# The end of the last group in a four-layer graph network: new order of the last steps, gate before theta, bias by TensorE, flag read before the last store

## The chip, the cores and the metric

The kernel runs on one core of a Trainium2 chip. The core's engines are TensorE (PE in the profile; PEld is its weight load), VectorE (DVE), ScalarE (ACT), GpSimd (POOL) and SyncE (SP, which issues the transfers here). Each engine works off its own queue in order and waits for the others at semaphores. The metric is the time of one execution on the device in microseconds.

## The reference, cut to what matters

There are 128 graphs of 64 nodes with 256 features each. Four blocks follow one another, each with layer norm ahead of it; `nodemask` is all ones.

```python
# block 0 and 1: attention over the graph with 8 heads, 32 wide
scores = q @ k.T / sqrt(32)           # block 0: masked by adj; block 1: + log(adj + 1e-6)
x = x + softmax(scores) @ v @ Wo + bo
# block 2: gated graph network, 5 steps
m = h @ weight[l];  agg = adj.T @ m
r, z = sigmoid(agg @ w_ih + h @ w_hh + biases)
n = tanh(agg_n + b + r * (h_n + b'));  h = (1 - z) * n + z * h
# block 3: gated mix of a filtered and a plain product
norm = (sum(|adj|) + 1e-6) ** -0.5
f_hom = adj @ (x @ theta * norm) * norm
f_het = x @ W_h
gate = sigmoid(x @ W_t + b_t)
out = x + elu(gate * f_hom + (1 - gate) * f_het)
```

The last lines are where most of the change lies: `theta`, `W_t` and `W_h` are three 256 x 256 matrices, and the elu closes the kernel.

## The kernel before, in words

The 128 graphs are paired into blocks of 128 rows, and four blocks make a group, so there are 16 groups, 0 to 15. A group passes through the front (both attention blocks), five steps of the gated network, and the back (block 3). The groups overlap: while one is in its five steps, the next one's front and the last one's back are mixed in. All arithmetic is float32.

The order on each engine is not written by hand. Every step is recorded with an engine, an estimated cost and the values that it reads and writes; a planner (`Plan.run`) then gives out one step at a time. Steps have a key, their due place in the run: it comes from the strand in which they were recorded (a base and a span, in units of groups) and is pulled forward by what depends on them. Of the steps of an engine that could begin within 15 ns of the first one, the planner takes the one with the lowest key. What it gives out is emitted in that order, and the engines keep it.

The names that matter here:

- `last_step` is the fifth step of the gated network, in token order, with banks `gb`, `nb`, `gc`, `nc` (L1195). For group 15 (`halves`) it finishes blocks 0 and 1, then blocks 2 and 3. Sums from the banks are made on VectorE (L1221), the last product of half 0 goes through ScalarE copies (L1230) and two additions of the bias row (L1233). `update` then does tanh of both gates together (L1254), L1255, L1257, tanh (L1259), L1260, L1265 and L1267, which gives `ht`.
- `back_half` is block 3 for two blocks: x gets `ht` (L1458), then statistics (L587, L588, L548), `rstd` as a power on POOL (L549), `xn` (L593), a transposition on TensorE (`lnT`, L563) and `hT` on ScalarE (L568).
- `plain_products` gives, for each block, `f` = x theta (L1396, copied by VectorE at L1403) and `gate`, a bank with both the gate's and the plain product (L1400, copied by ScalarE at L1404).
- Then, for each block: bias `b_t` (L1476 on POOL for group 15, L1479 on VectorE otherwise), tanh (L1481), `hom`, the filtered product (L1483), and the elementwise steps L1486, L1489, L1491, L1497, L1502, L1504, L1506. L1508 stores two blocks, 256 KB. Group 14's half 0 is left for the end too, and is mixed with group 15.

The first program (`lean`) assumes that no row of the input of block 2 has a variance of exactly zero. A flag says whether that held (written at L1575); if not, a general program runs after it. The flag is read by all engines behind the whole first program:

```python
        network(tc, a, out, flag)
        beyond = nc.values_load(flag[0:1, 0:1])
        with tc.If(beyond > 0, preferred_fallthrough_block=False):
            network(tc, a, out, None)
```

In the built program of before, the blocks of code lie in this order: first program, the waits for the outstanding stores (the way out when the flag is 0), general program, end. The functions that the change touches:

Of the kernel before, what the change touches and what calls it, by code (L numbers as in the profile page):

```python
# [23 lines left out]
P = 128  # L24
# [45 lines left out]
LOCK = 0.26  # L70
BACK_END = 0.1
# [62 lines left out]
class Op:  # L134
    __slots__ = ("eng", "cost", "lat", "fn", "key", "left", "users", "ready", "vals", "port", "mode", "leaves")


class Plan:
# [3 lines left out]
    def __init__(self):  # L142
        self.ops, self.at = [], 0.0
# [10 lines left out]
    def add(self, eng, cost, fn, reads=(), writes=(), lat=None, early=0.0, holds=(), port=False, mode=WIDE, leaves=None):  # L154
# [5 lines left out]
        op.key = self.at - early  # L160
# [47 lines left out]
    def run(self):  # L208
# [12 lines left out]
        for _ in range(len(self.ops)):  # L221
# [3 lines left out]
            for eng, ops in ready.items():  # L225
# [16 lines left out]
                if found:  # L242
                    first = min(at for at, _ in found) + 15
                    small = sum(t[1].mode in (T64, T32) and t[0] <= first + 100 for t in found)
                    pick = min((t for t in found if t[0] <= first),
# [33 lines left out]
def gnn_stack_kernel(tc: tile.TileContext, a: dict, out: bass.AP):  # L279
    nc = tc.nc  # L280
    with tc.tile_pool(name="flag", bufs=1) as keep:
        flag = keep.tile([P, 1], mybir.dt.int32, name="flag")
        network(tc, a, out, flag)
        beyond = nc.values_load(flag[0:1, 0:1])
        with tc.If(beyond > 0, preferred_fallthrough_block=False):
            network(tc, a, out, None)
# [3 lines left out]
def network(ctx: ExitStack, tc: tile.TileContext, a: dict, out: bass.AP, flag):  # L290
# [896 lines left out]
    def last_step(nm, h, Th, Ta, agg, gv, banks, operand, by_both, whole, halves):  # L1187
# [37 lines left out]
        def taken(oc, half, which):  # L1225
            ps = slice(oc, PAIRS, 2) if halves else slice(2 * half, 2 * half + 2)
            for t in range(2):
# [16 lines left out]
        def update(j):  # L1244
# [6 lines left out]
            else:  # L1251
                hh = lambda: ht[:, :, j * P : (j + 1) * P]
                before, to = [(ht, j)], (ht, j)
            sca(act(2 * TOK, 0.4), lambda: nc.scalar.activation(sg.tile, sg.tile, AF.Tanh, scale=0.5), parts, [sg])  # L1254
            vec2(dve(TOK), lambda: nc.vector.scalar_tensor_tensor(  # L1255
                a_(), r(), 1.0, a_(), op0=ALU.add, op1=ALU.mult), [sg, sn], [sn])
# [6 lines left out]
            else:  # L1263
                pool(1230, less(nc.gpsimd), [*before, sn], [sn])
            vec2(dve(TOK), lambda: nc.vector.scalar_tensor_tensor(  # L1265
                b_(), z(), 1.0, b_(), op0=ALU.add, op1=ALU.mult), [sg, sn], [sn])
# [4 lines left out]
        if halves:  # L1271
# [4 lines left out]
            both(4, 0)  # L1276
            taken(1, 0, 0)
            update(0)
            both(5, 1, True)
            summed(1, 1, 1, v)  # L1280
            both(3, 1)
            summed(0, 1, 1, u)
            update(1)
            yield
# [81 lines left out]
    def back(g, xt, norm):  # L1366
# [20 lines left out]
        for half in (0, 1) if g + 1 == n_groups else (1, 0):  # L1387
            back_half(g, xt, adjT, norm, half)

    def plain_products(hT, F, name):  # L1390

        for i in range(2):
# [10 lines left out]
            vec(dve(256), lambda i=i, pf=pf: nc.vector.tensor_copy(F[i][:, 0, :], pf[:, :D]), [pf], [(F[i], 0)])  # L1403
# [49 lines left out]

    def back_half(g, xt, adjT, norm, half):
        h_by_token = final[g]
        for p in range(2 * half, 2 * half + 2):
# [5 lines left out]
        hT = normed(xt, half, f"{g}_3_{half}")  # L1462

        F = [new("F" if g + 2 < n_groups or half else "h" if g + 2 == n_groups else ("kexp", "qk")[i], [P, 3, D], 2, f"F_{g}_{2 * half + i}") for i in range(2)]
        if g + 1 == n_groups or g + 2 == n_groups and not half:
# [3 lines left out]
        for p in range(2 * half, 2 * half + 2):  # L1469
# [5 lines left out]
            if g + 1 == n_groups:  # L1475
# [135 lines left out]
```

## Time and profile before

| | before |
|---|---|
| time, median of 3 runs | 2499.57 us (2499.54 to 2500.3) |
| profiled execution, its own time | 2500.02 us |
| its span, first to last instruction | 2498.1 us |
| mean granted TensorE clock | 0.996 |
| busy: PE / DVE / ACT / POOL | 2472.3 / 1911.6 / 1300.1 / 1009.7 us |
| instructions | 58019 |
| last step on VectorE ends | 2491.19 us |

Times inside the run are microseconds from the first instruction. The span is what the instructions cover; the execution's own time is 1.9 us longer. A busy PE in the profile is not PE at its peak, since products are pipelined and their ends are modelled. In the chain of work that ended last, each piece is what released the next one. In lists of groups, `out<-in` names the tiles, and a releaser is what ended an engine's wait.

### The profile page before, as it was taken

How to read it: one execution, taken by the hardware profiler on the slowest of the kernel's cores; microseconds unless marked ns; L12 is line 12 of the kernel's file. 1: busy time of each engine (PE TensorE's matmuls, PEld its weight loads, DVE VectorE, ACT ScalarE, POOL GpSimd, SP SyncE). 2: the span in 40 equal slices, each digit the busy share in tenths (PEclk: the TensorE clock that was granted, in tenths of full speed). 3: DMA queues.
4: the chain of work that ended last, by engine and by line, in shares of the span. 5: the costliest groups of instructions: out<-in, count | busy, mean ns of one | idle time of the engine just before them, and what ended most of it. 6: DMA issues, size and time to landing. Idle time of an engine off the chain costs nothing.

```text
span 2498.1 us, 58019 instructions
## 1 busy us (share of the span) xinstructions
PE 2472.3 (99%) x23481; PEld 2030.7 (81%) x23481; DVE 1911.6 (77%) x4524; ACT 1300.1 (52%) x2634; POOL 1009.7 (40%) x959
## 2 busy tenths in 40 slices
PE   9999999999999999999999999999999999999997
PEld 7788888887878878788888888878788787887874
DVE  5567787878777787877878778787877878867777
ACT  3355555555555555455555555555554555654544
POOL 5633424435243352533535244352433525234342
PEclk9999999999999999999999999999999999999998
DMA  7422212212222121222213132122222212212210
GB/s 219 155 81 86 75 50 95 77 50 87 72 80 70 62 83 63 80 70 84 76 48 104 50 102 74 55 77 72 80 70 69 73 62 80 74 49 70 72 50 19
DMA packets 88603, 191.45 MB, mean 77 GB/s; under 512 B 23603, under 2 KB 77189, under 8 KB 77445
## 3 DMA queue, kind: packets, MB, share of 16 engines
q1 hardware_dynamic: 88208, 187.59, 22.5%
q8 instruction: 188, 3.08, 0.5%
q14 instruction: 91, 0.74, 0.1%
q10 hardware_dynamic: 116, 0.04, 0.0%
HBM read 169.58 MB, written 18.02 MB: 75 GB/s over the span
## 4 chain that ended last, share of the span: by engine, by line
PE 97%; DVE 2%; ACT 1%; POOL 0%; issue 0%; DMA 0%; DVEq 0%; ACTq 0%
PE gb L1013 18%; PE gc L1013 13%; PE nb L1013 9%; PE nc L1013 7%; PE qkvb L727 6%; PE qkvc L727 5%; PE y L895 4%; PE nb L1195 3%; PE agg L1058 3%; PE gb L1195 3%; PE l3b L1425 3%; PE s L791 3%; PE gc L1195 3%; PE nc L1195 2%; PE l3c L1425 2%; PE hT L563 2%
## 5 line engine op out<-in xcount | busy, mean ns | idle before, releaser
L1127 POOL TENSOR_TENSOR sn<-h,sn 128x512 f32<-128x512 f32 x128 | 164.4, 1284 | 542.2 <-ACT sn L1125 542.2
L815 POOL TENSOR_TENSOR e<-e,mask 128x512 f32<-128x512 f32 x128 | 170.2, 1342 | 237.9 <-ACT e L813 237.9
L982 POOL TENSOR_TENSOR Th<-h 128x256 f32<-128x256 f32 x160 | 125.5, 803 | 272.4 <-PE nb L1013 133.1
L1013 PE MATMUL gb<-Ta,gv 128*128 128x256 f32 x768 | 199.0, 381 | 0.3 <-DVE Ta L1071 0.3
L1013 PE MATMUL gb<-Th,w_hh 128*128 128x256 f32 x768 | 197.4, 380 | 0.7 <-DVE sg L1090 0.7
L549 POOL TENSOR_TENSOR rstd<-pw,few 128x2 f32<-128x2 f32 x128 | 114.2, 892 | 206.3 <-DVE pw L548 202.9
L1013 PEld LDWEIGHTS gb<-Ta,gv 128*128 128x128 f32 x768 | 141.5, 190 | 21.9 <-DVE Ta L1071 0.7
L1125 ACT ACTIVATE sn<-sn,b_n 128x512 f32<-128x512 f32 x128 | 92.1, 720 | 129.1 <-DVE sn L1123 127.6
L1013 PEld LDWEIGHTS gb<-Th,w_hh 128*128 128x128 f32 x768 | 140.3, 190 | 20.1 <-issue 1.2
L1071 DVE TENSOR_TENSOR Ta<-agg 128x256 f32<-128x256 f32 x160 | 93.9, 589 | 79.5 <-ACT sg L1117 37.0
L1129 DVE SCALAR_TENSOR_TENSOR sn<-sg,sn 128x512 f32<-128x512 f32 x128 | 115.8, 905 | 45.9 <-POOL sn L1127 45.1
L982 POOL TENSOR_TENSOR Th<-h,Th 128x256 f32<-128x256 f32 x160 | 134.9, 843 | 8.9 <-DVE h L1131 5.9
L895 PE MATMUL y<-w_L_gnn_Wo,oT 128*128 128x256 f32 x512 | 133.3, 380 | 0.1
L1013 PE MATMUL gc<-h,w_hh 128*128 128x256 f32 x512 | 131.9, 380 | 0.1
L1013 PE MATMUL gc<-agg,gv 128*128 128x256 f32 x512 | 131.4, 379 | 0.0
L804 POOL TENSOR_TENSOR x<-x,r_L_gnn_bo 128x512 f32<-128x512 f32 x64 | 89.4, 1397 | 77.9 <-DVE xn L593 52.5
L568 ACT ACTIVATE hT<-lnT 128x512 f32<-128x512 f32 x96 | 57.2, 596 | 116.9 <-PE lnT L563 116.9
L1064 ACT ACTIVATE agg<-agg 128x512 f32<-128x512 f32 x160 | 86.6, 593 | 58.9 <-PE agg L1058 58.8
L1013 PE MATMUL nb<-Th,w_hh 128*128 128x256 f32 x384 | 116.1, 384 | 0.0
L1013 PE MATMUL nb<-Ta,gv 128*128 128x256 f32 x384 | 114.5, 380 | 0.0
L727 PEld LDWEIGHTS qkvb<-hTQ,qw 128*128 128x128 f32 x696 | 100.0, 191 | 16.6 <-DVE v L748 0.8
L1090 DVE TENSOR_TENSOR sg<-gc,ug 128x512 f32<-128x512 f32 x64 | 43.8, 685 | 89.4 <-PE gc L1013 88.2
(286 smaller groups left out, 7122.9 us busy)
## 6 DMA issues: line engine op xcount, KB each, us to landing
gv<-gates SPq DMA_DIRECT2D x80, 1344.0 KB, 5.8
qw<-kept SPq DMA_DIRECT2D x203, 192.0 KB, 2.4
x<-in_x_dram SPq DMA_DIRECT2D x32, 256.0 KB, 3.6
out_dram<-x SPq DMA_DIRECT2D x32, 256.0 KB, 2.2
gates<-gv SPq DMA_DIRECT2D x5, 1344.0 KB, 5.1
adjq<-in_adj_dram SPq DMA_DIRECT2D x8, 256.0 KB, 3.5
adjblk<-in_adj_dram SPq DMA_DIRECT2D x32, 64.0 KB, 2.3
gw<-in_L_gnn_weight_dram SPq DMA_DIRECT2D x5, 256.0 KB, 6.8
```

Source lines behind the costliest of these rows:

```text
L549: pool(660 if n == 2 else 970, lambda: nc.gpsimd.tensor_tensor(dst.tile, s.tile, few[:, 1 : 1 + n], op=ALU.pow), [s, (few, 1)], [dst], port=2)
L727: nc.tensor.matmul(bk[:, j * P : (j + 1) * P], lhs, rhs, start=first and j == 0, stop=True, skip_group_check=True)
L815: pool(1225, lambda e=e: nc.gpsimd.tensor_tensor(e.tile, e.tile, bias_at(pp)[:, None, :].to_broadcast([P, 4, 2 * NODES]), op=ALU.mult), [e ...
L895: pe(mm(256), lambda i=i, c=c: nc.tensor.matmul(py[:, i * D : (i + 1) * D], oT[:, i, c, :], w_o[:, c, :], start=c == 0, stop=c == 1), [(oT ...
L982: pool(690, lambda: nc.gpsimd.tensor_tensor(T[:, i, :], x(), y(), op=ALU.subtract), reads, [(T, i)])
L1013: nc.tensor.matmul(bank_[:, col * HALF : (col + 1) * HALF], at(g, n), rhs(), start=first and j == 0, stop=True, skip_group_check=True)
L1071: vec2(dve(256), lambda: nc.vector.tensor_tensor(Ta[:, i, :], x(), y(), op=ALU.subtract), reads, [(Ta, i)])
L1125: sca(act(TOK, 1.5), lambda: nc.scalar.activation(a_(), a_(), AF.Tanh, bias=b_n[:, oc : oc + 1]), [n_v, b_n], [n_v])
L1127: pool(1230, lambda: nc.gpsimd.tensor_tensor(b_(), hh(), a_(), op=ALU.subtract), [*hp, n_v], [n_v])
L1129: vec2(dve(TOK), lambda: nc.vector.scalar_tensor_tensor(b_(), z(), 1.0, b_(), op0=ALU.add, op1=ALU.mult), [*ts[1], n_v], [n_v])
L1195: pe(mm(384), lambda t=t, bk=bk: nc.tensor.matmul(bk[:, P:] if of_h else bk[:, : 3 * P], b()[:, t * P : (t + 1) * P], w[:, :, n, :], start ...
L1425: pe(mm(384), lambda: nc.tensor.matmul(bk[:, : 3 * P], b(), w3[:, :, n, :], start=first, stop=True, skip_group_check=True), [w3, *reads], ...
```

## The change

The change concerns group 15, the part of group 14 that is left for the end, and the way out of the program.

- The two halves of group 15's back are recorded in strands of their own (`END`, `END_SPAN`), and steps recorded with `plan.wait = 200` let the planner take a step with a lower key even where it can begin only up to 200 ns after the first possible one. This is set for `taken`, `update` and the norm of group 15's back.
- The last product of half 0 in `last_step` is added to its bias row directly from the bank by VectorE, and tanh of r and of z are two instructions.
- `last_half` takes the place of the products and elementwise steps for group 15: the bias goes into the gate's bank by a product with a column of the identity; both blocks' gate products come ahead of both blocks' theta products; tanh and the plain product are read from the bank; `part` = (1 - gate) * plain and (1 + tanh) * norm are made apart, so that after `hom` there are one product, one addition, exp, and two steps onto x, from which 1 has been taken before. Half 0's `f` is copied by ScalarE, half 1's by VectorE.
- Group 14's half 0 uses the same formula with the bias still on POOL, its `f` copied by ScalarE.
- The last store is split: block 2, then block 3. The flag is read ahead of the last store, and the general program's code lies ahead of the waits for the stores (`preferred_fallthrough_block=True`). The built order of code is: first program, general program, waits for the stores, end.

```diff
+END = 1.85, 1.9
+END_SPAN = 0.5, 0.5
+ENDS = 1
+WAIT = 200
...
-                    first = min(at for at, _ in found) + 15
-                    small = sum(t[1].mode in (T64, T32) and t[0] <= first + 100 for t in found)
-                    pick = min((t for t in found if t[0] <= first),
+                    first = min(at for at, _ in found)
+                    small = sum(t[1].mode in (T64, T32) and t[0] <= first + 115 for t in found)
+                    pick = min((t for t in found if t[0] <= first + t[1].wait),
                                key=lambda t: t[1].key + self.shift(mode, t[1].mode, small))
...
-        network(tc, a, out, flag)
-        beyond = nc.values_load(flag[0:1, 0:1])
-        with tc.If(beyond > 0, preferred_fallthrough_block=False):
+        beyond = network(tc, a, out, flag)
+        with tc.If(beyond > 0, preferred_fallthrough_block=True):
             network(tc, a, out, None)
...
+            for t in range(2) if halves else ():
+                bk, p = banks[which][t], 2 * t + oc
+                for dst, part in zip(s[half], (slice(1, 3), slice(0, 4, 3))):
+                    vec(dve(256), lambda dst=dst, part=part, bk=bk, p=p: nc.vector.tensor_tensor(
+                        dst[:, p], bk.tile.rearrange("p (g f) -> p g f", g=4)[:, part, :], b_row[:, oc, part, :], op=ALU.add),
+                        [bk, b_row], [(dst, p)])
+            if halves:
+                return
...
+            rz = [(sg, k) for k in "rz"] if halves else [sg, sg]
+            if halves:
+                for k in range(2):
+                    sca(act(TOK, 0.4), lambda k=k: nc.scalar.activation(
+                        sg[:, :, k, :], sg[:, :, k, :], AF.Tanh, scale=0.5), parts, [rz[k]])
+            else:
+                sca(act(2 * TOK, 0.4), lambda: nc.scalar.activation(sg.tile, sg.tile, AF.Tanh, scale=0.5), parts, [sg])
...
+            plan.wait = WAIT
             taken(1, 0, 0)
             update(0)
+            plan.wait = 15
...
-        for half in (0, 1) if g + 1 == n_groups else (1, 0):
+        if g + 1 == n_groups:
+            return adjT
+        for half in 1, 0:
...
-            vec(dve(256), lambda i=i, pf=pf: nc.vector.tensor_copy(F[i][:, 0, :], pf[:, :D]), [pf], [(F[i], 0)])
+            sca(act(256), lambda i=i, pf=pf: nc.scalar.activation(F[i][:, 0, :], pf[:, :D], AF.Copy), [pf], [(F[i], 0)])
...
+    def last_half(g, xt, hT, F, adjT, norm, half):
+        blocks = range(2 * half, 2 * half + 2)
+        pg, pf = ([new_(f"{n}_{g}_{p}") for p in blocks] for n, new_ in (("gate", gate), ("f", bank)))
+        for p in blocks:
+            sca(act(256, 0.4), lambda p=p: nc.scalar.activation(
+                xt[:, p, :], xt[:, p, :], AF.Copy, bias=-1.0), [(xt, p)], [(xt, p)])
+        for i in range(2):
+            pe(mm(256), lambda i=i: nc.tensor.matmul(
+                pg[i][:, :D], ident[:, 0:1].to_broadcast([P, P]), b_t.tile, start=True, stop=True,
+                skip_group_check=True), [ident, b_t], [pg[i]], holds=[F[i]])
+        for i in range(2):
+            for kc in range(2):
+                pe(mm(512), lambda kc=kc, i=i: nc.tensor.matmul(
+                    pg[i].tile, hT[:, kc, i * P : (i + 1) * P], w3[:, 1:, 2 * kc : 2 * kc + 2, :], start=False, stop=True,
+                    skip_group_check=True), [hT, w3], [pg[i]])
+        for i in range(2):
+            for kc in range(2):
+                pe(mm(256), lambda kc=kc, i=i: nc.tensor.matmul(
+                    pf[i][:, :D], hT[:, kc, i * P : (i + 1) * P], w3[:, 0, 2 * kc : 2 * kc + 2, :],
+                    start=kc == 0, stop=kc == 1), [hT, w3], [pf[i]])
+        for i, p in enumerate(blocks):
+            f, gt = (lambda i=i, k=k: F[i][:, k, :] for k in range(2))
+            sca(act(256, 0.4), lambda i=i, gt=gt: nc.scalar.activation(gt(), pg[i][:, :D], AF.Tanh, scale=0.5),
+                [pg[i]], [(F[i], 1)])
+            if half:
+                vec(dve(256), lambda i=i, f=f: nc.vector.tensor_copy(f(), pf[i][:, :D]), [pf[i]], [(F[i], 0)])
+            else:
+                sca(act(256), lambda i=i, f=f: nc.scalar.activation(f(), pf[i][:, :D], AF.Copy), [pf[i]], [(F[i], 0)])
+            pe(mm(256), lambda i=i, p=p, f=f: nc.tensor.matmul(
+                pf[i][:, D:], adjT[:, p, :], f(), start=True, stop=True), [adjT, (F[i], 0)], [pf[i]])
+            part = new("cp", [P, D], 5, f"part_{g}_{p}")
+            sca(act(256, 0.4), lambda gt=gt, part=part: nc.scalar.activation(
+                part.tile, gt(), AF.Copy, scale=-0.5, bias=0.5), [(F[i], 1)], [part])
+            vec(dve(256), lambda i=i, part=part: nc.vector.tensor_tensor(
+                part.tile, pg[i][:, D:], part.tile, op=ALU.mult), [pg[i], part], [part])
+            sca(act(256, 2), lambda p=p, gt=gt: nc.scalar.activation(
+                gt(), gt(), AF.Identity, scale=norm[:, p : p + 1], bias=norm[:, p : p + 1]),
+                [(F[i], 1), norm], [(F[i], 1)])
+            o = new("o", [P, D], 2, f"o3_{g}_{p}")
+            vec(dve(256), lambda i=i, o=o, gt=gt: nc.vector.scalar_tensor_tensor(
+                o.tile, pf[i][:, D:], 0.5, gt(), op0=ALU.mult, op1=ALU.mult), [pf[i], (F[i], 1)], [o])
+            vec2(dve(256), lambda o=o, part=part: nc.vector.tensor_tensor(
+                o.tile, o.tile, part.tile, op=ALU.add), [o, part], [o])
+            sca(act(256, 0.4), lambda o=o, gt=gt: nc.scalar.activation(gt(), o.tile, AF.Exp), [o], [(F[i], 1)])
+            vec2(dve(256), lambda p=p, o=o: nc.vector.scalar_tensor_tensor(
+                xt[:, p, :], o.tile, 0.0, xt[:, p, :], op0=ALU.max, op1=ALU.add), [o, (xt, p)], [(xt, p)])
+            vec2(dve(256), lambda p=p, gt=gt: nc.vector.scalar_tensor_tensor(
+                xt[:, p, :], gt(), 1.0, xt[:, p, :], op0=ALU.min, op1=ALU.add), [(F[i], 1), (xt, p)], [(xt, p)])
+        if not half:
+            dma(256, lambda: nc.sync.dma_start(
+                out_t[:, g * PAIRS : g * PAIRS + 2, :], xt[:, :2, :]), [(xt, 0), (xt, 1)], [])
+            return
+        dma(128, lambda: nc.sync.dma_start(out_t[:, g * PAIRS + 2, :], xt[:, 2, :]), [(xt, 2)], [])
+        ends.append((xt, 3))
+        if not lean:
+            last_store()
...
-        if g + 1 == n_groups or g + 2 == n_groups and not half:
+        if g + 1 == n_groups:
+            last_half(g, xt, hT, F, adjT, norm, half)
+            return
+        if g + 2 == n_groups and not half:
             plain_products(hT, F, f"{g}_{half}")
...
+            if ENDS and g + 2 == n_groups and half == 0:
                 pool(650, lambda gt=gt: nc.gpsimd.tensor_tensor(gt(), gt(), b_t.tile, op=ALU.add),
                      [(v, 0), (v, 1), b_t], [(v, "gt")])
...
+                part = new("cp", [P, D], 5, f"part_{nm}")
+                sca(act(256, 0.4), lambda gt=gt, part=part: nc.scalar.activation(
+                    part.tile, gt(), AF.Copy, scale=-0.5, bias=0.5), [(v, "gt")], [part])
+                pool(690, lambda het=het, part=part: nc.gpsimd.tensor_tensor(
+                    part.tile, het(), part.tile, op=ALU.mult), [part, (v, 0), (v, 1)], [part])
+                sca(act(256, 2), lambda p=p, gt=gt: nc.scalar.activation(
+                    gt(), gt(), AF.Identity, scale=norm[:, p : p + 1], bias=norm[:, p : p + 1]),
+                    [(v, "gt"), norm], [(v, "gt")])
+                vec(dve(256), lambda o=o, ph=ph, gt=gt: nc.vector.scalar_tensor_tensor(
+                    o.tile, ph[:, :D], 0.5, gt(), op0=ALU.mult, op1=ALU.mult), [ph, (v, "gt")], [o])
+                vec2(dve(256), lambda o=o, part=part: nc.vector.tensor_tensor(
+                    o.tile, o.tile, part.tile, op=ALU.add), [o, part], [o])
+                sca(act(256, 0.4), lambda o=o, gt=gt: nc.scalar.activation(gt(), o.tile, AF.Exp), [o], [(v, "gt")])
+                vec2(dve(256), lambda p=p, o=o: nc.vector.scalar_tensor_tensor(
+                    xt[:, p, :], o.tile, 0.0, xt[:, p, :], op0=ALU.max, op1=ALU.add), [o, (xt, p)], [(xt, p)])
+                vec2(dve(256), lambda p=p, gt=gt: nc.vector.scalar_tensor_tensor(
+                    xt[:, p, :], gt(), 1.0, xt[:, p, :], op0=ALU.min, op1=ALU.add), [(v, "gt"), (xt, p)], [(xt, p)])
+                continue
...
+    read = []
+
+    def last_store(known=None):
+        xt, p = ends.pop()
+
+        def go():
+            if lean:
+                read.append(nc.values_load(flag[0:1, 0:1]))
+            nc.sync.dma_start(out_t[:, n_pairs - PAIRS + p, :], xt[:, p, :])
+
+        dma(128, go, [(xt, p)] + ([known] if lean else []), [])
+
+    ends = []
...
-                back(g, *held.pop(g))
+                xt, norm = held.pop(g)
+                adjT = back(g, xt, norm)
+            for half in range(2) if last else ():
+                with plan.strand(begin[g] + END[half], END_SPAN[half]):
+                    back_half(g, xt, adjT, norm, half)
...
+        with plan.strand(n_groups + 2.0, 0.1):
+            last_store(known)
     plan.run()
+    return read[0] if lean else None
```

## Prediction

> **What bounds the kernel now.** First the page's chain of work that ended last, by engine:
>
> ```profile
> PE 97%; DVE 2%; ACT 1%; POOL 0%; issue 0%; DMA 0%; DVEq 0%; ACTq 0%
> ```
>
> TensorE carries it, and the listed orders of instructions of the two kernels are the same on every engine until the last 60 us, two ScalarE steps near 2435 apart. So only the end can change. A table of that end by windows (window, its length, then busy us of PE, PEld, DVE, ACT, POOL; granted clock; DMA share and GB/s):
>
> ```profile
> 2430.00:2460.00 30.00, 29.89 (x164) 18.36 (x163) 24.91 (x50) 16.07 (x32) 15.66 (x13) 1.00 0.03 10
> 2460.00:2470.00 10.00, 4.23 (x14) 2.20 (x12) 9.40 (x25) 3.53 (x6) 1.75 (x1) 0.94 0.00 0
> 2470.00:2480.00 10.00, 9.28 (x27) 5.80 (x28) 6.51 (x21) 3.46 (x7) 1.55 (x3) 0.72 0.08 29
> ```
>
> Until 2460 PE is full; from 2460 to 2470 it idles, VectorE is full (9.40 of 10), and the clock pays afterwards (0.72). What fills those 10 us, from the chain in order of time (start, us, what):
>
> ```profile
> 2462.83 0.06 DVE x L1458
> ...
> 2467.69 1.76 POOL rstd L549
> ...
> 2471.20 0.61 ACT hT L568
> ...
> 2471.85 2.07 PE f L1396 x4
> 2473.92 2.65 PE gate L1400 x4
> 2476.58 0.86 PE f L1396 x4
> 2477.44 1.72 PE gate L1400 x4
> ...
> 2480.71 1.13 PE f L1396 x4
> ...
> 2486.14 0.45 PE hom L1483 x2
> ...
> 2490.77 0.42 DVE x L1506
> ```
>
> The same f and gate groups take 4.72 us after the idle stretch and 2.58 later. After the last hom (2486.59) 4.6 us of elementwise work remain, until 2491.19. Then the exit (engine and operation of a line: durations in ns, first to last start):
>
> ```profile
> L1508 SPq DMA_DIRECT2D out_dram<-x x32: 372/389/394, 370.7 to 2491.2; - x32
> ...
> L284 SPq TENSOR_LOAD <-flag x1: 479/479/479, 2491.6 to 2491.6; - x1
> ...
> L285 SPq COMPARE_BRANCH  x2: 43/46/49, 2492.2 to 2494.2; - x2
> ...
> L1607 SPq EVENT_SEMAPHORE  x10: 17/28/28, 2496.8 to 2498.1; - x10
> ```
>
> Last store, flag, a branch that falls through, the waits for the stores (2.9 us to landing in the DMA view of 2490 to 2500), then at 2494.2 a branch over the fallback network: SP's next instruction is at 2496.8, 2.5 us later. From the last DVE end (T = 2491.2) to the span's end: 6.9 us.
>
> **The change part by part.** I walk the listed order of each engine with durations of before. Units: PE 0.43 us for a 256-column product, 0.65 for 384, 0.86 for 512; DVE 0.42 for 256 elements (next start after 0.34), 0.68 for 512 (after 0.60, a dependent one after 0.78); ACT 0.42, 0.63 (512, tanh); POOL pow 0.71; PE's result reaches DVE or ACT 0.2 after its slot, other hand-overs 0.04 to 0.1.
>
> *GRU, half 0.* The pairs L1195 are permuted, not changed: they end at 2455.63 as before, the last gb and nb 0.65 earlier, at 2453.05 and 2453.69. Removed: four ACT copies (L1230) and two DVE additions of 512. Added: four DVE additions from the bank, 2453.3 to 2454.7. Tanh of r alone ends at 2455.0 (before: 1.06 us for both, to 2456.74). Then L1255 2455.06, L1257 2455.84, tanh 2456.56 to 2457.19, L1260 2457.45 behind three sums of half 1, L1265 2458.23, L1267 2459.01: ht at 2459.7 against 2462.5. The x, statistics and pow's input of half 0 now stand directly behind: x 2459.95 and 2460.35, statistics from 2460.76, pow's input done 2461.9 (before 2467.6, because update and products of half 1 were mixed in), rstd 2462.7.
>
> *What is passed over.* The four sums of half 1 (L1221, from u) stand after that; nc ends 1.7 us later than before (2462.1 against 2460.4), since two bias products (0.86) and theta's (0.86) are ahead of it, and the sums end at 2463.4. xn at 2463.3 and 2463.65, lnT at 2464.7 to 2465.1. The other two bias products reuse gc's and nc's banks, so they wait for those sums, and lnT is queued behind them; the sums end before xn, so this costs nothing; were the sums later, lnT would move with them one for one. All four bias products (1.7 us) lie before PE's wait for half 0; without that cover they cost 1.7. Group 14's POOL addition stands ahead of rstd: it ends at 2461.5, 0.4 before rstd is wanted.
>
> *hT of half 0* stands on ACT behind two subtractions on x15 (which wait for xn) and a copy of group 14: 2465.45 to 2466.05. PE idles 0.6, then gates 3.44, theta 1.72, hom of group 14 0.43, two hom 0.86, with 0.1 to restart: 2472.6. The f group starts at 2471.85 before, this gate group at 2466.1: 5.7 us earlier, and with no idle stretch near the 3.4 us that led to the 0.72 clock.
>
> *Half 1.* r's tanh 2463.5, L1255 2464.05, L1257 to 2465.53, but its tanh stands on ACT behind hT of half 0 and runs 2466.05 to 2466.68; L1260 2466.72, L1265 2467.5, L1267 to 2469.0, x and statistics to 2470.95, rstd 2471.8, xn to 2472.8 (one addition and one product of other blocks before it, in rstd's shadow), lnT to 2473.4, two subtractions on ACT, then hT to 2474.05. PE is done with half 0 at 2472.6, so both engines arrive about together, and an error of half a microsecond on either shows. Gates of blocks 2 and 3 to 2477.6, theta to 2479.4, the last copy 2480.0, the last hom 2480.55. Before, each of these blocks went gate copy 0.60, POOL bias 0.72, tanh 0.42, and after hom L1486, L1489, L1491, L1497, L1502, L1504, L1506, seven steps. Now tanh reads the bank, and part and the factor with norm are done under theta; the gate's second half is multiplied straight from the bank. After the last hom: product 2480.96, addition 2481.69 (between steps of the block before), exp 2482.2 to 2482.6, last step 2482.7: T = 2483.1. Two terms I raise: pow at its mean 0.89 instead of the median 0.71 (+0.18, for half 1 alone: half 0's has 0.6 to spare), a restart after a gap by 0.27 as in the 1.13 against 0.86 (+0.17). T = 2483.5, 7.7 earlier.
>
> *ACT's added work* (two subtractions, a copy, part, per block) lies in gaps of an engine with 3.5 busy us in 10; group 14's two, placed near 2435 ahead of an l5 copy, cost 0 to 0.8, where DVE's user of that copy comes much later: 0. The copies of theta moved from DVE to ACT: 0 net.
>
> *Exit.* The flag was written at 2332.5, so SP's load of it ahead of the last store waits for nothing and vanishes behind the wait for x; the other engines load it after their last step, as before. The second store of group 14 and the two earlier ones of group 15 stand ahead on SP, and their data are done by 2480.5. The last store carries 128 KB instead of 256. The blocks are swapped: fallback first, the waits for stores behind it. The branch at T + 0.5 now jumps, 2.5 us, while the store lands (2.2 to 2.9 from T): T + 3.0; eight semaphores at 0.073, T + 3.6; the end block follows in line, 1.3 as before: T + 5.0, 1.9 less. DVE's jump takes longer (2491.6 to 2495.0, 3.4) and ends at T + 3.6, within that. No row shows this order: bounds are a second jump (+2.5, so 0.6 worse than before) and a store and jump in full overlap with the semaphores (2.5 better); I take 1.9, by the rows of both pieces. [...] The row has 0.05 where it falls through and 2.5 where it jumps. [...] Before has such a jump too, after the landing, so the count stays one.
>
> *Sum.* Span 2483.5 + 5.0 = 2488.5. The profiled run is 2500.02 for a span of 2498.1 (1.9 outside): 2490.4, and it lies 0.45 over the median of the three runs, 2499.57: 2490.0.
>
> **Rivals.** *Early start lost* (chance 0.12). POOL or ACT in front of rstd or hT of half 0 is late, and PE begins near 2471.85 with the cold 2.1 us. Then 2471.85 + 2.1 + 12.0 of both halves' products + 0.9 (hom of group 14, lnT) + 0.3 waiting for the last copy gives the last hom at 2487.1, and the 2.55 behind it T = 2489.7: 2496.1, of the gain only tail and exit. For it: DVE steps beside POOL's two-input ones stretch (L1491 955 ns mean instead of 420). Against: POOL has only 4 x 0.72 and two pow there, so at most 4.3 us.
>
> *Exit gains nothing or jumps twice* (0.10): 0 to 0.6 over before's exit, 2491.9 to 2492.5. For it: no run shows the layout. Against: one branch of before falls through at 0.05.
>
> *Slow clock* (0.03), the other side: PE has several short waits from 2463 on, and the clock stays at about half for the whole last stage, as in the f group's 2.07 against 0.86. The stage holds some 13 us of products; at half rate T = 2496, 2502.5. It decides once the slow work passes 10 of those 13 us. Against: the gap of 2.4 us at 2463.5 cost the next hom nothing, and mine are below 1 us.
>
> That the change does not do what it says is out: the listed order shows every move.
>
> **How the numbers follow.** Forecast 0.75 (2488 to 2493), the rivals 0.12, 0.10, 0.03. Measurement tells 0.2%, 5.0 us, from no change: 2494.6. Forecast and exit rival lie below it; of the lost start three quarters lie above: same 0.09. Slower needs over 2504.6: the slow clock's upper part and what I do not see, 0.02. Range 2487.5 to 2494.5: lower end if every raised term and the full exit overlap go my way, upper end towards the lost start.
>
> **What would show it.** Right: lnT of group 15's half 0 near 2465, gate of its block 0 near 2466, granted clock near 1 from 2465 to 2480, the last DVE step near 2483.5 with SP's end block 3.7 later. Wrong: PE waiting over 3 us for hT, rstd behind a late POOL step, two jumps on SP, or an end of the L1195 pairs after 2456.

## The result, and the profile after

| | before | after |
|---|---|---|
| time, median of 5 runs each | 2499.57 us | 2488.49 us (2488.33 to 2489.63) |
| ratio | | 0.9957, 95% interval 0.9942 to 0.9971 |
| profiled execution, its own time / span | 2500.02 / 2498.1 us | 2488.33 / 2486.5 us |
| last step on VectorE ends (T) | 2491.19 us | 2481.34 us |
| T to the end of the span | 6.9 us | 5.15 us |
| write of the flag to the end of the span | 165.6 us | 155.7 us |

The changed kernel is 11.1 us faster; 2490.0 was forecast. The last row is the better measure of the change. The after trace runs 1.67 us ahead of the before trace from about 11 us on, long before anything that the change touches, and keeps that lead as far as the flag (written at 2332.5 and 2330.8). So of the 11.6 us between the two spans 1.67 belong to the start, told at the end, and about 10 to the change. Put on the scale of before, T is 2483.0.

The stretches of the end again, in the table by windows (busy us of PE, PEld, DVE, ACT, POOL; granted clock; DMA share, GB/s):

```profile
2460.00:2470.00 10.00, 9.75 (x35) 5.83 (x34) 9.25 (x24) 9.22 (x21) 3.88 (x5) 1.00 0.09 29
2470.00:2480.00 10.00, 8.16 (x29) 4.64 (x27) 9.15 (x26) 6.01 (x15) 0.23 (x1) 1.00 0.16 55
2480.00:2492.00 12.00, 0.00 (x0) 0.00 (x0) 1.23 (x4) 0.42 (x1) 0.00 (x0) 0.80 0.09 29
```

TensorE's hole is gone (9.75 busy of 10 instead of 4.23), the clock stays at 1.00 (0.72 before), and TensorE is done before 2480. The chain in order of time (start, us, what):

```profile
2462.30 0.86 PE gate L1484 x4
2463.16 0.45 PE lnT L566 x4
...
2463.64 0.61 ACT hT L571
...
2464.29 3.70 PE gate L1489 x8
2467.99 1.73 PE f L1494 x8
...
2471.64 0.61 ACT hT L571
...
2472.29 3.70 PE gate L1489 x8
2475.99 1.74 PE f L1494 x8
...
2477.76 0.42 DVE F L1502
...
2480.91 0.43 DVE x L1523
```

Each half takes 5.4 us of products at full clock, one `hT` of 0.6 us ahead of each, and 3.2 us of VectorE steps follow the last copy of theta (L1502). The exit (engine and operation of a line: durations in ns, first to last start):

```profile
L1630 SPq TENSOR_LOAD <-flag x1: 512/512/512, 2480.9 to 2480.9; - x1
...
L1631 SPq DMA_DIRECT2D out_dram<-x x1: 348/348/348, 2481.5 to 2481.5; - x1
...
L288 SPq EVENT_SEMAPHORE  x8: 17/17/17, 2484.6 to 2485.1; - x8
...
L288 PEldq COMPARE_BRANCH  x1: 3585/3585/3585, 2478.8 to 2478.8; - x1
...
L288 SPq COMPARE_BRANCH  x1: 45/45/45, 2481.9 to 2481.9; - x1
```

There is one branch per engine instead of two. SP's jumps at 2481.9, while the last 128 KB are under way, and SP goes on at 2484.6; the eight waits for stores behind it, 17 ns each, find everything landed. The load of the flag did not vanish wholly: it stands behind block 2's store, which waits for block 2's last step, so the last store leaves 0.2 after T.

### The profile page after: what moved, and what is told of

Same layout as the page of the kernel before. It is cut to its first block, busy times and chain, and to the rows that moved or that the text cites. A ratio compares the mean times of both kernels' runs of the same rounds, so it can differ in the third digit from the quotient of the medians.

```text
span 2486.5 us, 58043 instructions
## 1 busy us (share of the span) xinstructions
PE 2470.6 (99%) x23489; PEld 2030.3 (82%) x23489; DVE 1906.9 (77%) x4518; ACT 1302.6 (52%) x2644; POOL 1006.8 (40%) x959
## 4 chain that ended last, share of the span: by engine, by line
PE 97%; DVE 1%; ACT 1%; issue 0%; POOL 0%; DMA 0%; DVEq 0%; ACTq 0%
PE gb L1016 18%; PE gc L1016 13%; PE nb L1016 9%; PE nc L1016 7%; PE qkvb L730 6%; PE qkvc L730 5%; PE y L898 4%; PE nb L1198 3%; PE agg L1061 3%; PE gb L1198 3%; PE l3b L1448 3%; PE s L794 3%; PE gc L1198 3%; PE nc L1198 3%; PE l3c L1448 2%; PE hT L566 2%
```

## The experiments

The first four kernels are the kernel before with one part of the change, the others the changed kernel with one part undone or moved. The kernel before ran beside each batch, on three chips: medians 2499.07 (49 runs, beside e1 to e4), 2499.07 (21, beside e5 to e8) and 2498.64 (9, beside e9 to e12). The changed kernel ran in none of these batches, and the intervals of e6 to e12 overlap its own (0.9942 to 0.9971). So a difference of about 1 us between two of these kernels is read from the traces; the medians only hint at it.

The span of every run is known, and its median leaves out the time around the span (1.8 to 2.4 us). The last two columns are read from the one trace of each kernel, count from the write of the flag, and so leave the start out; T is again the end of the last VectorE step. "Flag to end" also contains SP's last jump, which took between 2.6 us (before) and 3.5 us (e7) from trace to trace, so for the work ahead of the exit "flag to T" is the better measure.

| kernel | median us (runs) | median span | ratio, 95% interval | flag to T | flag to end |
|---|---|---|---|---|---|
| before | 2499.07 (49) | 2497.2 | | 158.7 | 165.6 |
| changed | 2488.49 (5) | 2486.6 | 0.9957, 0.9942 to 0.9971 | 150.5 | 155.7 |
| e1_exit | 2497.13 (13) | 2495.3 | 0.9994, 0.9986 to 1.0002 | 158.6 | 164.2 |
| e2_layout | 2497.49 (13) | 2495.7 | 0.9995, 0.9987 to 1.0003 | 158.4 | 164.2 |
| e3_urgent | 2498.76 (13) | 2497.0 | 1.0000, 0.9991 to 1.0008 | 160.4 | 167.7 |
| e4_form | 2495.49 (21) | 2493.6 | 0.9986, 0.9979 to 0.9993 | 155.0 | 161.3 |
| e5_no_urgent | 2493.72 (15) | 2491.9 | 0.9979, 0.9971 to 0.9987 | 154.7 | 160.4 |
| e6_theta_first | 2489.16 (5) | 2487.1 | 0.9960, 0.9946 to 0.9974 | 151.2 | 156.4 |
| e7_no_sums | 2489.46 (5) | 2487.7 | 0.9961, 0.9948 to 0.9975 | 151.4 | 157.5 |
| e8_warm | 2491.25 (7) | 2489.4 | 0.9969, 0.9958 to 0.9981 | 153.3 | 158.7 |
| e9_bias_dve | 2489.46 (5) | 2487.4 | 0.9965, 0.9952 to 0.9979 | 150.5 | 156.2 |
| e10_old_exit | 2490.01 (5) | 2487.7 | 0.9964, 0.9951 to 0.9978 | 150.5 | 157.0 |
| e11_bias_later | 2488.78 (5) | 2486.7 | 0.9961, 0.9947 to 0.9974 | 150.3 | 155.7 |
| e12_start | 2489.48 (5) | 2487.1 | 0.9962, 0.9949 to 0.9976 | 150.5 | 155.7 |

### The exit alone, and its layout alone

The kernel before, with the changed layout and, in e1_exit only, the flag loaded in `network` ahead of the last store (of 256 KB here). e1_exit:

```diff
-        network(tc, a, out, flag)
-        beyond = nc.values_load(flag[0:1, 0:1])
-        with tc.If(beyond > 0, preferred_fallthrough_block=False):
+        beyond = network(tc, a, out, flag)
+        with tc.If(beyond > 0, preferred_fallthrough_block=True):
```

In e2_layout the last line alone is changed.

> The kernel before with the way out of the change alone: flag read ahead of the last store (still 256 KB), general program's code ahead of the waits for stores. Counted from the flag's write on VectorE to the end of the span, before has 165.6 us (2332.5 to 2498.1) and the changed kernel 155.7. Theory (the 2.5 us jump now runs beside the store's landing): from the last DVE end to the end of the span 5.1 us in place of 6.9, so 163.8 from the flag's write, 1.8 us of time. [...] Rival 2 (a second jump is needed behind the waits): 166.2.

> The kernel before with the general program's code ahead of the waits for stores, and the flag read behind the last store as before. Theory: SP issues the store until T + 0.4, loads the flag until T + 0.9, jumps until T + 3.6, waits through eight semaphores until T + 4.2, end block 1.3: T + 5.5 in place of 6.9, so 164.2 us from the flag's write, and 0.4 of the exit's 1.8 us are the flag's place. Rival (the gain is the flag's place, the code's order gives nothing): 165.6, no change.

Both end 1.4 us sooner from the flag (1.9 and 1.6 by the medians, each of whose intervals reaches 1, no change). From T to the end e1 takes 5.7 and e2 5.8, where before takes 6.9, so most of the gain is the layout. What the flag's place adds is open: reading it ahead moved SP's branch from 1.0 to 0.5 after T, but in these two traces the jump then took 3.3 us instead of 2.9, and both spans end at 2495.1. By the medians e1 is 0.4 ahead, the size that was expected, with runs of each spread over 2 us.

### The order alone

The kernel before, with `plan.wait` at 200 around `update`, x and `normed` of group 15, and the halves' own strands:

```diff
+            plan.wait = WAIT
...
+                with plan.strand(begin[g] + END[half], END_SPAN[half]):
+                    back_half(g, xt, adjT, norm, half)
```

> The kernel before with the order by urgency alone: strands of their own for the last group's two halves and the planner's wait of 200 ns; formulas, bias on POOL, gate after theta and exit as before. Theory (the 10 us of idle PE were an order of VectorE's queue that mixes half 1's update into half 0's norm): lnT of half 0 some 4 us earlier than 2470.0, granted clock near 1 after it, last DVE step 4 to 5 us earlier: 160.6 to 161.6 us from the flag's write. Rival (TensorE's products of the last stage are what fills the end, and the formulas shorten it): 164.6 to 165.6.

Missed by both theories: nothing gained in the median, and 2.1 us lost in the profiled execution, which was the slowest of its 13 (2500.53; the range begins at 2497.01). The order does what it says: `lnT` of half 0 starts at 2462.8, as in the changed kernel. But the gain is given back at the end, as a timeline of the last stretch shows:

```profile
2481.85 1.89 PE L1603 MATMUL hom<-F,adjT 128*128 128x256 f32 x8
...
2482.48 0.92 DVE L1606 SCALAR_TENSOR_TENSOR o<-hom,norm,F 128x256 f32<-128x256 f32 x2 [1.73 <-PE hom L1603]
...
2486.97 0.87 DVE L1606 SCALAR_TENSOR_TENSOR o<-hom,norm,F 128x256 f32<-128x256 f32 x2
...
2490.64 0.76 DVE L1626 SCALAR_TENSOR_TENSOR x<-o,x 128x256 f32<-128x256 f32 x2
```

With the old formulas the planner puts the four `hom` products of group 15 (two records each) behind all products of half 1. So the closing steps of all four blocks stand in one row on VectorE, 8.9 us from 2482.5 to 2491.4, where before only two blocks were left behind the last `hom` (4.5 us). And TensorE, though early, runs slow twice:

```profile
2460.00:2470.00 10.00, 8.08 (x22) 4.32 (x21) 9.59 (x28) 3.79 (x6) 0.95 (x2) 0.83 0.00 0
2470.00:2480.00 10.00, 8.15 (x24) 4.78 (x23) 5.78 (x16) 3.98 (x10) 1.87 (x3) 0.83 0.05 16
```

Each half begins with eight products in 4.3 us that take 2.6 at full clock, 1.7 lost each time. The thirteen runs lie in three groups: one at 2497.01 (mean clock 0.998), nine from 2498.59 to 2499.0 (0.997) and three from 2500.35 to 2500.53 (0.996 or 0.997). They lie about 1.7 us apart, the loss of one slow stretch, which fits no such stretch, one and two; only the slowest run has a trace, so that is an estimate.

### The formulas alone, and everything but the order

e4_form is the kernel before with `last_half`, the shortened steps of group 14's half 0 and the sums straight from the banks; order and exit stay. e5_no_urgent is the changed kernel with the planner's 15 and the old strand for both halves:

```diff
-WAIT = 200
+WAIT = 15
...
-        if g + 1 == n_groups:
-            return adjT
-        for half in 1, 0:
+        for half in (0, 1) if g + 1 == n_groups else (1, 0):
```

> The kernel before with the formulas of the change alone: last_half, group 14's half 0, sums straight from the bank, tanh of r and z apart; planner's wait, strands and exit as before. Theory: the tail behind the last hom 2.0 us shorter, the update up to 1 us shorter, the start of half 0 otherwise where it was: 162.6 to 163.6 us from the flag's write. Rival (the formulas carry the change, because they take VectorE and POOL steps out of the 10 us of idle PE): 158 to 159.

> The changed kernel with its order undone: the steps of the last group's update, normalisation and halves take their places as in the kernel before, the new formulas and the new exit stay. Measure: from the write of the flag on DVE to the span's end, 155.7 us in the changed kernel, 165.6 before. Theory A, order and formulas need each other: as in the run of the formulas alone, the gates of half 0 start about 4 us later, TensorE idles 3 us ahead of them and the clock then takes 5.2 us for 3.5 us of products. 161.3 of that run less 1.4 for the exit: 159.9, and a time near 2493.5. Rival B, each part is worth what it gave alone (order 0.3): 156.0, time near 2488.9.

e4 came out between its theory and the rival, 4.4 us better than before from the flag. Its theory gave half 0 at most 1 us of an earlier start; in the trace half 0's products start 1.7 us sooner, counted from the flag. The trace also flatters it: this execution (2494.06) was one of the fastest of 21 (median 2495.49, highest 2497.49), and its clock is at half for 3.4 us where that of before is for 6.8.

e5 is near its theory A in both numbers. So the order, worth 0.3 us by the medians in the kernel before, is worth 5.2 in the changed one (2493.72 less 2488.49), or 4.2 from the flag to T: the parts do not add. The chain of e5 (L1496 gate):

```profile
2468.84 5.12 PE gate L1496 x8
...
2477.08 3.49 PE gate L1496 x8
```

Counted from the flag, half 0 starts 4.2 us later than in the changed kernel (2468.84 less 2331.2, against 2464.29 less 2330.8), and its gate products take 5.12 us where half 1's take 3.49.

### The idle stretch filled

e5_no_urgent, plus turns in the transposition that gives `lnT`:

```diff
         def turn():
+            for _ in range(26 if name == "lnT_15_3_0" else 0):
+                nc.tensor.transpose(ps[:, :P], ident.tile, ident.tile)
```

> The kernel of the undone order (e5) plus 26 turns of the unit matrix on TensorE (2.8 us at full clock, 0.107 each) into the bank of half 0's lnT, right ahead of that lnT and overwritten by it. It adds only work in the idle stretch. Theory A, the slow gate products behind the stretch come from the idle TensorE: with it filled, the gate products of half 0 run at 0.43 each and the end comes 1.6 to 1.8 us sooner than in e5: 158.2 from flag to end, time near 2491.8. Rival B, the slow products come from what VectorE or the banks do there: as e5, or later by what the turns push lnT.

The chain of this kernel (its L1498 is the gate line):

```profile
2464.22 2.84 PE lnT L567 x26
...
2468.65 3.70 PE gate L1498 x8
```

Theory A holds in kind. Turns that compute nothing new stand in the hole, the gate products behind them start at the same time as in e5 and take 3.70 instead of 5.12. What slowed them was TensorE's own idle time. The mean clock is 0.999 in six of the seven runs, and 0.998 or less in all fifteen of e5. T comes 1.4 us sooner than in e5, which is what the gate products gained; the end comes 1.7 sooner, 0.3 of it from a shorter jump of SP (by the medians 2.5). So of the 4.2 us to T that the order is worth, 1.4 are the clock and 2.8 the earlier start itself.

### Theta first; the sums by copies; the bias on VectorE

In e6_theta_first the two loops of `last_half` change places:

```diff
-        for i in range(2):
-            for kc in range(2):
-                pe(mm(512), lambda kc=kc, i=i: nc.tensor.matmul(
-                    pg[i].tile, hT[:, kc, i * P : (i + 1) * P], w3[:, 1:, 2 * kc : 2 * kc + 2, :], start=False, stop=True,
-                    skip_group_check=True), [hT, w3], [pg[i]])
         for i in range(2):
             for kc in range(2):
                 pe(mm(256), lambda kc=kc, i=i: nc.tensor.matmul(
                     pf[i][:, :D], hT[:, kc, i * P : (i + 1) * P], w3[:, 0, 2 * kc : 2 * kc + 2, :],
                     start=kc == 0, stop=kc == 1), [hT, w3], [pf[i]])
+        for i in range(2):
+            for kc in range(2):
+                pe(mm(512), lambda kc=kc, i=i: nc.tensor.matmul(
...
```

In e7_no_sums `taken` and `update` keep their old way for `halves` (the copies on ScalarE, two additions of 512, one tanh):

```diff
-            if halves:
-                return
...
-            if halves:
-                for k in range(2):
-                    sca(act(TOK, 0.4), lambda k=k: nc.scalar.activation(
-                        sg[:, :, k, :], sg[:, :, k, :], AF.Tanh, scale=0.5), parts, [rz[k]])
```

In e9_bias_dve the bias products go, the gate products start their banks themselves, and VectorE adds:

```diff
-                pg[i][:, :D], ident[:, 0:1].to_broadcast([P, P]), b_t.tile, start=True, stop=True,
...
-            sca(act(256, 0.4), lambda i=i, gt=gt: nc.scalar.activation(gt(), pg[i][:, :D], AF.Tanh, scale=0.5),
-                [pg[i]], [(F[i], 1)])
+            vec(dve(256), lambda i=i, gt=gt: nc.vector.tensor_tensor(gt(), pg[i][:, :D], b_t.tile, op=ALU.add),
+                [pg[i], b_t], [(F[i], 1)])
+            sca(act(256, 0.4), lambda gt=gt: nc.scalar.activation(gt(), gt(), AF.Tanh, scale=0.5),
+                [(F[i], 1)], [(F[i], 1)])
```

> The changed kernel with theta's four products ahead of the four gate products in both halves of the last group, all else as changed. Theory A: in half 1 the gates' banks are full 1.7 us later, tanh, part and the factor with norm then stand behind the last product instead of beside theta, and the last VectorE step moves by 0.8 to 1.5: from flag to end 156.7, time near 2489.5. Rival B: the end is bound by VectorE's own steps (9.15 us busy of the 10 from 2470), which stay as many: 155.7, no change.

> The changed kernel with the sums of the update's half 0 as before: ScalarE copies the banks, VectorE adds, one tanh for r and z together. Theory A: ht of half 0 comes 2 to 2.8 us later, TensorE idles so long ahead of the gates of half 0, and the clock may fall behind it: from flag to end 157.7 without a fall of the clock, 159.5 with it; time 2490.5 to 2492.3, I take 2491.5. Rival B: the chain through ht has that much slack against pow and the earlier groups' steps: 156.2 at most.

> The changed kernel with the bias of the last group's gates added by VectorE from the bank into SBUF (four steps of 256 elements), tanh reading that, and no bias products on TensorE. Theory A: the four products of TensorE lie beside other work and cost nearly nothing, while VectorE (9.2 busy us of 10 in both stretches from 2460 to 2480) has no room: four steps of 0.34, one of them between the last gate bank and its tanh, and the end comes 0.3 to 1.0 later: time near 2489.1 against 2488.5. Rival B: the two products right ahead of half 0's lnT hold it for 0.6 (xn is ready at 2462.4, lnT starts at 2463.0), and without them the end comes 0.4 sooner: near 2488.1.

**e6** is 0.7 slower by the medians, at T and at the end: theory A, a little under its lower bound of 0.8.

**e7** is 1.0 slower by the medians and 0.9 later at T. The 1.8 from flag to end have another 0.9 in them from SP's jump, which took 3.5 us in this one execution where it took 2.6 in the changed kernel. Theory A had 2 to 4, B 0.5. `ht` of half 0 came only 1.3 later, and `xn` only 0.5: in the changed kernel `rstd` is ready at 2460.9, but `xn` stands on VectorE behind sums of half 1 until 2461.6, while in e7 it follows `rstd` directly (2462.0 and 2462.1). `lnT` comes 0.4 later, and the clock did not fall (1.00).

**e9** is 1.0 slower in the median. Two of its five runs are 1.4 us or more above the others at a mean clock of 0.998, which is also that of e11's profiled execution with its slow start, so the median says little. In the trace half 0's gates start 1.0 sooner than in the changed kernel, as rival B said, but 0.8 of that is lost again before half 1's, and T is the same. The end is 0.5 later: the last step of block 2 is now late, SP's load of the flag stands behind block 2's store, and so the last store leaves 0.7 after T instead of 0.2. Theory A has the sign, but the loss that the trace shows lies in the exit and not on VectorE; B's 0.6 is there without reaching the end.

### The old exit in the changed kernel

```diff
-        with tc.If(beyond > 0, preferred_fallthrough_block=True):
+        beyond = nc.values_load(flag[0:1, 0:1])
+        with tc.If(beyond > 0, preferred_fallthrough_block=False):
```

> The changed kernel with the exit of the kernel before: flag loaded behind the last store, waits for the stores ahead of the branch that jumps. The blocks 2 and 3 keep their own stores of 128 KB. Theory A: the jump comes after the landing again; from the last VectorE step to the span's end 6.3, as in the run of the formulas alone, against 5.15: time near 2489.6. Rival B, the exit is worth what it gave in the kernel before (1.9 by the medians): near 2490.4. Rival C, worth nothing here since the landing of 128 KB is short: 2488.5.

T to the end 6.5 instead of 5.15, the time 1.5 slower (1.1 by the spans): theory A in kind, its size between A and B. Of the 1.3 in the trace 0.5 is a longer jump (3.1 us instead of 2.6), so these two traces don't give the exact price. SP branches twice again (its lines: the branch instructions, then the waits):

```profile
L292 SPq EVENT_SEMAPHORE  x8: 17/17/17, 2482.4 to 2483.0; - x8
...
L292 SPq COMPARE_BRANCH  x2: 42/46/49, 2482.3 to 2483.1; - x2
```

The stores have landed by 2483.0, and the jump at 2483.1 is fully open.

### Two tries at something better

In e11_bias_later the planner gets one more dependence for half 1's bias products, on the `lnT` bank of their half, which moves these two products and nothing else but one `hom` of group 14 into their place:

```diff
-                skip_group_check=True), [ident, b_t], [pg[i]], holds=[F[i]])
+                skip_group_check=True), [ident, b_t, *(turned[-1:] if half else [])], [pg[i]], holds=[F[i]])
```

e12_start has six turns ahead of the first `lnT`, and six behind it into a bank of their own:

```diff
         def turn():
+            for _ in range(6 if name == "lnT_0_0_0" else 0):
+                nc.tensor.transpose(ps[:, :P], ident.tile, ident.tile)
```

> The changed kernel with one move on TensorE alone: the two bias products of half 1 go from ahead of half 0's lnT to behind half 1's lnT, where TensorE waits 0.96 us for hT; the last product of group 14 takes their place. Theory A: lnT of half 0 starts 0.4 sooner, but hT stands on ScalarE behind a copy that ends at 2463.54 and so starts only 0.1 sooner than 2463.64; the products fit into the wait of half 1: end 0 to 0.2 sooner, time 2488.3 to 2488.5. Rival B: hT follows lnT, and the end comes 0.4 to 0.6 sooner, near 2488.0.

> The changed kernel with 12 more turns of the unit matrix on TensorE in the first 8 us: six ahead of the first lnT (idle from 5.1 to 6.0 in the profile of before) and six behind it (idle from 6.7 to 7.6). Theory A: where the first products run at half clock (7.6 to 11.1 in the profile of before, 1.67 us lost), it is since TensorE did little in the stretch ahead[...]; with the idle filled every run starts like the fastest: median 2488.3, and the spread of the runs falls from 1.3 to under 0.6. Rival B: the slow start is drawn at random, whatever TensorE does: spread as before, median 2488.5 to 2488.9.

**e11**: `lnT` of half 0 starts 0.4 sooner (its trace shifted by the flag's 1.5), half 0's gates and T 0.2, and the end from the flag is the same 155.7; the median differs by 0.3 in the wrong direction. Theory A, worth nothing that can be measured.

**e12** failed. The first products run at full clock in its trace, but of the six turns ahead of the first `lnT` two and part of a third still ran at half clock and pushed it (6.60 instead of 6.06, and the first product from 7.62 to 7.89). The median is 1.0 above that of the changed kernel (0.5 by the spans), and the runs spread over 1.1 us, so neither theory's numbers hold. No version here beats the change.

## Why the prediction was right, point by point

- **What bounds.** TensorE, with one hole from 2460 to 2470 and a slow clock behind it: both went, as said. e5 and e8 show that the slow clock was a consequence of the hole, worth 1.4 us at T.
- **Half 0.** On the scale of before: pairs end at 2455.64 (2455.63 forecast), `lnT` starts at 2464.67 (2464.7), gates at 2465.96 (2466.1). The walk through the listed orders was good to 0.15 us over the whole half.
- **Half 1.** `hT` ends at 2473.9 (2474.05), gates start at 2473.96. TensorE was done with half 0 at 2472.5 (2472.6), so it waited about 1.0, a little more than the forecast's "about together".
- **The last steps.** T is 2483.0 against 2483.5, and 2483.1 without the two raised terms. The raises were the mis-sized terms: the power of half 1 took 0.81 (taken as 0.89), and the first product behind each wait 0.70 instead of 0.59, 0.10 of restart where 0.27 was taken.
- **Bias "costs nothing".** Nearly. The two products ahead of `lnT` held it by 0.6, since `xn` was earlier than TensorE; e11 puts the price of the two at 0.2 at T and none at the end.
- **Exit, 1.9.** 1.8 by T to the end of before and after, whose jumps are equally long; 1.3 alone in e1, and 1.3 in the changed kernel (e10), where jumps of other lengths are mixed in. The jump lies beside the landing as said (SP's from 2481.9 to 2484.6, the last store issued at 2481.5). One detail failed: the last store left at T + 0.20, not at once, because the load of the flag waits behind block 2's store. Whether the early read of the flag brings anything by itself stays open (e1 against e2).
- **Parts.** The sum was made for the whole, and there it holds. Read as a list of parts it would not: 1.9, 0.3 and 3.6 us alone, 5.8 in sum, against 10.6 of the whole kernel by the medians (2499.07 of the 49 runs less 2488.49). Order without the formulas piles the closing steps on VectorE; formulas without the order leave the hole and the slow clock.
- **The median.** 2488.49 against 2490.0. Half a microsecond is T. Of the rest a part is the start: the sum was hung on an execution of before that had drawn the slow one (2500.02, where 49 runs have a median of 2499.07), which the prediction corrected by 0.45 only. The changed kernel may have been lucky too: all five of its runs have a mean clock of 0.999, while in e9 and e11 two runs of five are slower at 0.998, as with a slow start.
- **The rivals.** No early start was lost, no engine jumped twice, the clock did not fall (1.00 from 2460 to 2480). The last was nearer than its chance says, and the argument against it, the length of single pauses, does not hold: with the order alone the clock fell twice behind pauses of at most 1.24 us (shown at the end).

## What to carry to other kernels

A hole on the engine that bounds cost twice here, 2.8 us of later start and 1.4 us of slow products behind it (e5 and e8): close such a hole with order, and count the slow products as part of its price. Where it stayed open, work that computes nothing bought the 1.4 us back (e8), while in e12 such work pushed the first `lnT` by 0.5 us. Cost a bundle of changes as one walk through the listed order, not as a sum of parts, since an order can be worth nothing until the formulas leave room behind it. And at the exit, put the jump where a transfer is still landing: the layout alone took 1.1 us off the way from T to the end (e2, 5.8 instead of 6.9). A kernel's one trace is one draw: the length of the jump and the slow start moved it by 0.9 and 1.7 us here, as much as single parts of the change were worth.

## What the runs showed of the hardware that was not expected

**The start differed from run to run.** The same 20 turns and the same first products ran in the profiles of before and after, by windows, before first:

```profile
6.00:8.00 2.00, 1.27 (x6) 0.76 (x7) 1.12 (x4) 0.60 (x1) 0.70 (x1) 0.96 1.06 277
8.00:10.00 2.00, 2.00 (x7) 1.61 (x6) 0.76 (x4) 0.00 (x0) 1.01 (x1) 0.50 1.01 345
```

and after:

```profile
6.00:8.00 2.00, 1.25 (x6) 0.81 (x7) 1.18 (x6) 0.60 (x1) 0.70 (x1) 1.00 1.06 297
8.00:10.00 2.00, 2.00 (x13) 1.69 (x11) 1.39 (x6) 0.00 (x0) 1.01 (x1) 1.00 1.06 389
```

TensorE was as busy in both, yet before ran at 0.50 and did 7 products where after did 13; 1.67 us came of it. In before full clock was granted at 4.4, in after at 5.8, and in before it was lost again at 7.8, for 3.4 us. Of the fourteen traces only two lost it there, those with the earliest grants: before, and e11 (granted at 4.1). Their flags are written at 2332.5 and 2332.3, those of the other twelve, granted at 5.0 to 7.3, at 2330.6 to 2331.4.

**The clock fell for 3.4 us or twice that while TensorE had work, in e3 behind short pauses.** In before it was at half from 2468.9 to 2475.7, twice 3.4 us (first row); in e3 from 2464.6 to 2468.0 and from 2474.8 to 2478.2 (next two):

```profile
2468.90:2475.60 6.70, 4.88 (x11) 3.04 (x12) 5.54 (x18) 2.68 (x6) 0.54 (x1) 0.50 0.00 1
...
2464.60:2467.90 3.30, 3.30 (x7) 1.94 (x6) 3.20 (x8) 1.05 (x2) 0.00 (x0) 0.50 0.00 0
...
2474.85:2478.20 3.35, 3.19 (x6) 2.19 (x7) 1.72 (x5) 1.33 (x5) 0.00 (x0) 0.50 0.01 2
```

In before the clock fell 2.2 us into a pause of TensorE of 3.40 us, which followed one of 2.40. In e3 the pauses of TensorE ahead of the two slow stretches were shorter (in brackets, with what ended them):

```profile
2462.83 0.78 PE L570 MATMUL lnT<-ident,xn 128*128 128x128 f32 x4 [1.24 <-DVE xn L600]
2464.30 1.84 PE L1423 MATMUL f<-w,hT 128*128 128x256 f32 x4 [0.69 <-ACT hT L575]
...
2473.06 0.33 PE L570 MATMUL lnT<-ident,xn 128*128 128x128 f32 x1 [0.78 <-DVE xn L600]
2473.78 0.55 PE L570 MATMUL lnT<-ident,xn 128*128 128x128 f32 x3 [0.39 <-DVE xn L600]
2475.01 1.22 PE L1423 MATMUL f<-w,hT 128*128 128x256 f32 x2 [0.69 <-ACT hT L575]
```

None is over 1.24 us, and at the start of before, between the grant at 4.4 and the loss at 7.8, TensorE paused for 0.81 and 0.69. How much idle time it takes in all, and why the clock fell behind some pauses and not behind others, no run here settles.

**A taken jump took 2.6 to 4.2 us** on SP and PE, from run to run: over the fourteen traces SP's took 2.6 to 3.5 and PE's 3.3 to 4.2 (the row of the changed kernel has 3585 ns), while a branch that fell through took about 0.05 on SP (43 to 49 ns in before). **The landing of a store varied as well:** block 2's 128 KB took 1.7 us from its issue in the changed kernel and 2.6 in e6, the last 256 KB 2.9 in before and 3.2 in e1, and the 256 KB stores of before as a whole 2.1 to 3.8.
